# Attention kernel: row sums of weights pass through DRAM with the values, channel means are written to DRAM from their own tile

## The chip, the cores and the metric

The kernel runs on one core of one Trainium2 chip. The metric is the device time of one execution, in microseconds (us). The kernel before takes 2475.26 us, the median of three runs (2474.96 to 2476.18). All data are fp32.

## The reference

Two layers work on `x` of shape 16 x 1024 x 256 (batches, nodes, channels). Layer 0 is a graph layer: x is aggregated over a normalized adjacency, goes through a linear layer, a batch norm, a relu, a second linear layer and a second batch norm, is added to x, and is layer-normed. Layer 1, where the change is made, gates the adjacency by the nodes' channel means, makes queries from it and attends:

```python
fea = jnp.transpose(x, (0, 2, 1))
c_adj = jnp.mean(fea, axis=1)
diff = c_adj[:, None, :] - c_adj[:, :, None]
A = jnp.abs(jnp.abs(jax.nn.sigmoid(diff) - 0.5) - 0.5) * 2.0
A_s = (A + jnp.transpose(A, (0, 2, 1))) * 0.5
Wg = adj[None, :, :] * A_s
g = jnp.einsum('bcn,bnm->bcm', fea, Wg)
g = jax.nn.relu(g * para.reshape(1, C, N))
q = jnp.transpose(g, (0, 2, 1)).reshape(B, N, h, hd).transpose(0, 2, 1, 3)
kv = (x @ kv_w).reshape(B, N, 2, h, hd).transpose(2, 0, 3, 1, 4)
...
attn = jax.nn.softmax(jnp.einsum('bhnd,bhmd->bhnm', q, k) * scale, axis=-1)
out = jnp.einsum('bhnm,bhmd->bhnd', attn, v)
```

The result is added to x and layer-normed again. There are 4 heads of 64 channels.

## The kernel before

Layer 0 ends at about 815 us; the change doesn't touch it. Layer 1 is a software pipeline over 16 batches. A batch has 16 steps, in two halves of 512 queries each, and in each half two pairs of heads. A step makes the scores of 256 keys for one pair and one half (`scores`, L783), their exponentials on ScalarE (`exps`, L795), adds these up for the row sums on VectorE (`sums`, L801 and L804), and multiplies them with the values on TensorE (`attend`, L819).

Work for other batches is put between the steps. `put(b, t, f, ...)` sets a piece of work down for eighth t of batch b. The loop at L1161 takes two eighths at a time, which I call a block: first all pieces of both eighths in the order that `arrange` gives them, then four steps. Four blocks make a batch. In the block of eighths 0 and 1 of batch b lie the first gates, the keys and part of the values of batch b+1 (`gate`, `keys`, `values`) and the row sums of the second half of batch b-1; in that of 4 and 5 the row sums of the first half of batch b; in that of 6 and 7 the means and `crow` of batch b+2. Each engine runs its own instructions strictly in this order; every data transfer of this part is issued by SyncE in this order too, and a transfer that waits holds up those behind it.

Two paths matter here.

*Row sums.* When a half is through, its values (channels x queries, not yet divided) have gone to `o_dram` (L835). `dens` (L840) adds up the partial row sums over the partitions with a matmul against ones (L846), which leaves each head's sums 32 times over in a quarter of the partitions, and ScalarE copies them to DT (L848). `recips` turns them round with four TensorE transposes (L857), and VectorE writes the reciprocals to RD (L859). `fetch_o` (L872) reads the values from DRAM in such an order that VectorE's transpose of 32 x 32 blocks (L890) completes the turn to queries x channels; `finish_a` then multiplies with RD (L894), adds x (L899) and takes the moments of the layer norm, and `finish_b` applies it and writes the output. In most halves `finish_a` comes a block or more after its fetch. In the second half of batch 14 and the first of batch 15 it comes in the same block, the first of them after the third step. The second half of batch 15 (`by_pe`) doesn't pass through DRAM: TensorE transposes it.

*Channel means.* `means` (L674) scales the sums over channels in `css`, a tile of 128 x 8, one node for each number. The gates need them as one row of 1024, the same on all partitions. For the first batch TensorE makes it by transposes (L688). For the others `crow` transposes `css` on TensorE (L692), ScalarE copies the 8 x 128 result into a corner of the tile `crow` (L694), SyncE writes it to `c_dram` (L695), and reads that back to all partitions (L696). The first to read the tile is `wg_a` on ScalarE (L706), at the start of the next block. For batch 1 all this is part of the opening, where TensorE has no other work ahead.

PSUM has four buffers under the tag "t", taken in turn by keys, values, graph products, `pd`, `pr`, `pc` and the two accumulators of `attend`.

Of the kernel before, what the change touches and what calls it, by code (L numbers as in the profile page):

```python
# [22 lines left out]
def gnn_norm_attention_kernel(  # L23
# [57 lines left out]
    Q = 32  # L81
    NQ = P // Q
    y_blk = [yT_all[b].rearrange("i (d e) (q n) -> q e (i d) n", e=Q, q=NQ) for b in range(B)]
    o_dram = {(b, h): dram.tile([NT // NH, C, P], F32, name=f"o{b}_{h}") for b in range(B) for h in range(NH)}
    x1_dram = {
        (b, j): dram.tile([CT, 2 * P, P], F32, name=f"x1_{b}_{j}") for b in range(2, B) for j in range(NT // 2)
    }
# [479 lines left out]
    def fast():  # L567
      with ExitStack() as fx:
# [110 lines left out]
        def crow(b):  # L679


            crows[b] = crp.tile([P, N], F32, tag="crow", name=f"crow_{b}")
            if b == 0:
                for h in range(NH):
                    p = ps_t.tile([P, FB], F32, tag="t", name="pc")
                    for k in range(FB // P):
                        j = h * (FB // P) + k
                        nc.tensor.transpose(p[:, ts(k, P)], css[b][:, j : j + 1].to_broadcast([P, P]), ident)  # L688
                    nc.scalar.copy(crows[b][:, ts(h, FB)], p)
                return  # L690
            p = ps_t.tile([P, FB], F32, tag="t", name="pc")
            nc.tensor.transpose(p[:NT, :P], css[b], ident)  # L692
            t = crows[b][:NT, :P]
            nc.scalar.copy(t, p[:NT, :P])  # L694
            nc.sync.dma_start(c_dram[b], t)  # L695
            nc.sync.dma_start(crows[b], c_dram[b].rearrange("j p -> (j p)").partition_broadcast(P))  # L696


# [112 lines left out]
        def attend(g):  # L811
            b, hf, pair, cp = step(g)
            if cp == 0:
                O[b, hf, pair] = [ps_t.tile([P, FB], F32, tag="t", name=f"o{g}_{r}") for r in range(2)]
            for a in range(2):
                cb = 2 * cp + a
                for r in range(2):
                    for h in range(2):
                        nc.tensor.matmul(  # L819
                            O[b, hf, pair][r][h * HD : (h + 1) * HD, :],  # L820
                            vs[b][r * HD : (r + 1) * HD, cb, pair * P + h * HD : pair * P + (h + 1) * HD],
                            E[g, a][r * HD : (r + 1) * HD, h, :],
                            start=(cb == 0),
                            stop=(cb == NT - 1),
                        )
                E.pop((g, a))
            if cp == NT // 2 - 1:
                t = otp.tile([P, FB], F32, tag=f"ot{pair}", bufs=1, name=f"ot{g}")
                o = O.pop((b, hf, pair))
                nc.scalar.copy(t, o[0])  # L830
                nc.vector.tensor_add(t, o[1], t)  # L831
                if by_pe(b, hf):
                    OT[b, hf, pair] = t
                else:
                    nc.sync.dma_start(  # L835
                        o_dram[b, hf][:, ts(pair, P), :].rearrange("i p n -> p i n"),
                        t.rearrange("p (i n) -> p i n", n=P),
                    )

        def dens(b, hf):  # L840
            p = ps_t.tile([P, FB], F32, tag="t", name="pd")
            for pair in range(NP):
                acc = ACC.pop((b, hf, pair))
                for h in range(2):
                    k = 32 * (2 * pair + h)
                    nc.tensor.matmul(p[k : k + 32, :], ones32, acc[:, h, :], start=True, stop=True)  # L846
            DT[b, hf] = otp.tile([P, FB], F32, tag="dt", bufs=1, name=f"dt{b}_{hf}")
            nc.scalar.copy(DT[b, hf], p)  # L848


        R = {}
# [19 lines left out]

        def fetch_o(b, j):  # L872
            hf, k = divmod(2 * j, KB)
            t = OB[b, j] = otp.tile([P, 2, C], F32, tag="ob", bufs=2, name=f"ob{b}_{j}")
            blk = o_dram[b, hf].rearrange("i (d e) (q n) -> q e (i d) n", e=Q, q=NQ)
            for q in range(NQ):
                nc.sync.dma_start(
                    t[q * Q : (q + 1) * Q].rearrange("p a (d n) -> p (a d) n", n=Q),
                    blk[q][:, ts(k // 2, 2 * C // Q), :],
                )  # L880

        def finish_a(b, j):
            hf, k = divmod(2 * j, KB)
            pool_r = (rp, "r") if b < B - 1 else (x1p, "x1")
            r = pool_r[0].tile([P, 2, C], F32, tag=pool_r[1], name=f"r_{b}_{j}")
            if by_pe(b, hf):
                p = OB.pop((b, j))
            else:
                p = r
                nc.vector.transpose(  # L890
                    r.rearrange("p a c -> p (a c)"), OB.pop((b, j)).rearrange("p a c -> p (a c)")
                )
            rd = RD[:, b * NT + 2 * j : b * NT + 2 * j + 2, :].rearrange("p a h -> p (a h)")
            nc.vector.tensor_mul(  # L894
                r.rearrange("p a (h d) -> p (a h) d", h=HEADS),
                p.rearrange("p a (h d) -> p (a h) d", h=HEADS),
                rd.unsqueeze(2).to_broadcast([P, 2 * HEADS, HD]),
            )
            nc.vector.tensor_add(r, r, x1s.pop((b, j)))  # L899
            mv, rs = ln_stats(sm, r, f"z{b}_{j}")  # L900
            nm = sm.tile([P, 2], F32, tag="nm", name=f"nm_{b}_{j}")
            for a in range(2):
                nc.gpsimd.tensor_scalar(
                    nm[:, a : a + 1], mv[:, a, 0:1], rs[:, a : a + 1], -1.0, op0=OP.mult, op1=OP.mult
                )
            R[b, j] = (r, rs, nm)
# [49 lines left out]
        for b in range(B):  # L956

            for hf in range(NH):
                t = (hf + 1) * (NC // NH)
                put(b, t, dens, b, hf)  # L960
                put(b, t, recips, b, hf)
                for k in range(KB // 2):
                    j = hf * (KB // 2) + k

                    if b * NH + hf < B * NH - 3:
                        t_f, t_a, t_b = (t + 1, t + 2 + k, t + 6 + k) if hf == 0 else (t + 1, t + 4 + k, t + 6 + k)
                    elif not by_pe(b, hf):

                        t_f, t_a, t_b = t, t + 2 * k, t + 2 + 2 * k if b < B - 1 else (t + 2, NC + 1)[k]
                    else:  # L970
                        t_f, t_a, t_b = t, t + 1 + k, t + 2 + k
                    put(b, t_f, back if by_pe(b, hf) else fetch_o, b, j)
                    if t_a == t:
                        between[(b * NC + t) * 2 + NK // 2] = [(finish_a, (b, j))]
                    else:
                        put(b, t_a, finish_a, b, j)
                    put(b, t_b, finish_b, b, j)
# [58 lines left out]
        def arrange(pieces):  # L1036
            first = []
            gates = [fa for fa in pieces if fa[0] is gate]
            many = [fa for fa in pieces if fa[0] in long]
            first += [fa for fa in pieces if fa[0] is bn2_q]  # L1040
            alone = [fa for fa in pieces if fa[0] in (dens, back, recips, crow)]
            few = [fa for fa in pieces if fa not in first + gates + many + alone]
            few.sort(key=lambda fa: rank.get(fa[0], len(rank)))
            few_pe = [fa for fa in few if is_short(fa)]
            order = spread(many, few_pe) if len(many) < len(few_pe) else spread(few_pe, many)
            if few_pe and many and order[0][0] in long:
                order.remove(few_pe[0])
                order.insert(0, few_pe[0])

            for fa in few:  # L1050
                if not is_short(fa):
                    at_ = 0
                    for k, o in enumerate(order):
                        if o[0] in rank and rank[o[0]] <= rank.get(fa[0], len(rank)):
                            at_ = k + 1
                    order.insert(at_, fa)
            if any(fa[0] is graph for fa in many):
                order = gates + order
            else:
                order = spread(order, gates)  # L1060


            for fs, k in (((dens, back), 1), ((recips,), 2)):
                k = ([n for n, fa in enumerate(order) if fa[0] in long] + [len(order)] * 3)[k]
                order[k:k] = [fa for fa in alone if fa[0] in fs]
            return first + order + [fa for fa in alone if fa[0] is crow]


# [278 lines left out]
```

## Time and profile before

| | |
|---|---|
| time, median of 3 | 2475.26 us |
| span of the profiled execution | 2473.1 us |
| PE busy | 98% |
| DVE, ACT, POOL busy | 73%, 44%, 31% |
| DMA moved | 288.66 MB |
| transposes of row sums, L857 | 128, mean 274 ns |
| reciprocals from PSUM, L859 | 32, mean 242 ns; 15.8 us of waiting for `pr` |
| transposes of means, L692 | 15, mean 272 ns |
| fetches of values, L877 | 248 of 64 KB, 2.4 us to landing |
| `crow` broadcast, L696 | 15 of 512 KB, 3.7 us to landing |

PE is TensorE, PEld its weight loads, DVE VectorE, ACT ScalarE, POOL GpSimd, SPq the queue from which SyncE issues transfers. In the timeline, a line has the start of an instruction (or of a run of like ones), its time, engine, line of the kernel, operation, what it writes and reads, and in brackets how long the engine was idle before it and for whom. Names there are of tiles: `pr` is the transposed row sums, `pc` the transposed means, `pk`, `pv` and `pg` are keys, values and graph products, `s` scores, `e` exponentials, `o` attended values, `ob` the values as fetched, `st_d` a small DRAM tensor in which layer 0's last constants `s` and `t` are written at L600 to be fetched in another layout at L602.

### The profile page before, as it was taken

The page shows a single profiled execution, that of the slowest core. Times are in us where ns is not written, and L with a number is a line of the kernel's source. Part 1 is how long each engine was busy: PE and PEld are TensorE (multiplying, and loading weights), DVE is VectorE, ACT ScalarE, POOL GpSimd, SP SyncE. Part 2 cuts the span into 40 slices and gives each one's busy share as a digit, 9 for nine tenths or more (in the row PEclk, how much of TensorE's full clock was granted, in tenths as well). Part 3 has the DMA queues.
Part 4 walks back from the last instruction along what each step waited for, and adds up shares of the span by engine and source line. Part 5 has one row for each costly group of instructions (what it writes and reads, how often), then busy time and mean ns, then how long its engine had stood idle before and what let it go on. Part 6 is the DMA issues. An engine that isn't in the chain of part 4 may idle for free. (4 is left out here: it accounts for less than half of the span.)

```text
span 2473.1 us, 33867 instructions
## 1 busy us (share of the span) xinstructions
PE 2425.5 (98%) x12341; PEld 1021.1 (41%) x12341; DVE 1806.3 (73%) x2552; ACT 1095.1 (44%) x1549; POOL 767.2 (31%) x826
## 2 busy tenths in 40 slices
PE   8999999999999899999999999999999999999997
PEld 4444444444444443443434434344343443443432
DVE  5545545555776777888888878888888888888677
ACT  2000000002544455564655656656566465564645
POOL 2222232321656421313223133232332323414012
PEclk9999999999999899999999999999999999999999
DMA  4122222212677444544544535445354454544211
GB/s 136 68 85 102 78 86 92 102 68 85 226 266 260 125 120 90 129 128 104 141 111 108 144 87 145 116 115 147 76 147 108 118 145 92 135 114 113 65 40 53
DMA packets 563118, 288.66 MB, mean 117 GB/s; under 512 B 390664, under 2 KB 535680, under 8 KB 555776
## 3 DMA queue, kind: packets, MB, share of 16 engines
q1 hardware_dynamic: 562944, 286.43, 42.1%
q8 instruction: 99, 1.62, 0.3%
q14 instruction: 75, 0.61, 0.1%
HBM read 192.43 MB, written 93.91 MB: 116 GB/s over the span
## 5 line engine op out<-in xcount | busy, mean ns | idle before, releaser
L795 ACT ACTIVATE e<-s 128x1024 f32<-128x1024 f32 x512 | 496.1, 1020 | 338.0 <-PE s L783 286.3
L804 DVE TENSOR_TENSOR acc<-acc,e 128x1024 f32<-128x1024 f32 x384 | 517.1, 1347 | 116.6 <-ACT e L795 88.5
L783 PE MATMUL s<-qT,kT 64*64 64x512 f32 x4096 | 492.0, 595 | 3.5 <-ACT e L795 1.5
L819 PE MATMUL o<-e,v 64*64 64x512 f32 x4096 | 485.4, 589 | 0.0
L757 PE MATMUL pg<-wg,x 128*128 128x512 f32 x960 | 428.9, 597 | 0.0
L610 POOL TENSOR_TENSOR yt<-yt,stq 128x512 f32<-128x512 f32 x120 | 181.1, 1510 | 397.9 <-DMA yt<-yT 353.7
L819 PEld LDWEIGHTS o<-e,v 64*64 64x64 f32 x4096 | 156.6, 133 | 282.8 <-issue 274.3
L757 PEld LDWEIGHTS pg<-wg,x 128*128 128x128 f32 x960 | 177.7, 190 | 231.3 <-issue 229.1
L783 PEld LDWEIGHTS s<-qT,kT 64*64 64x64 f32 x4096 | 147.7, 133 | 296.2 <-issue 261.9
L103 ACT COPY u<-pa 128x512 f32<-128x512 f32 x15 | 8.8, 585 | 475.3 <-PE pa L308 475.3
L66 POOL TENSOR_SCALAR rs_z<-mv_z 128x2 f32<-128x2 f32 x64 | 18.3, 286 | 479.2 <-DVE mv_z L559 410.4
L716 DVE SCALAR_TENSOR_TENSOR wg<-wg,adj 128x1024 f32<-128x1024 f32 x128 | 163.5, 1308 | 3.0 <-DMA adj<-in_adj_dram 0.2
L308 PE MATMUL pa<-AhT,x 128*128 128x512 f32 x360 | 161.8, 592 | 0.0
L642 ACT ACTIVATE x<-x,nm_a,rs_a 128x256 f32<-128x256 f32 x128 | 75.8, 594 | 165.8 <-POOL nm_a L632 165.3
L831 DVE TENSOR_TENSOR ot<-o,ot 128x512 f32<-128x512 f32 x64 | 44.3, 692 | 139.2 <-ACT ot L830 139.2
L66 POOL TENSOR_SCALAR rs_a<-mv_a 128x2 f32<-128x2 f32 x64 | 39.4, 616 | 265.3 <-DVE mv_a L559 244.2
L732 PE MATMUL pk<-x1T,kvw 128*128 128x512 f32 x256 | 120.4, 605 | 0.0
L743 PE MATMUL pv<-kvw,x1T 128*128 128x256 f32 x512 | 118.4, 385 | 0.0
L339 PE MATMUL ph<-agg,SW 128*128 128x512 f32 x240 | 112.8, 592 | 0.0
L743 PEld LDWEIGHTS pv<-kvw,x1T 128*128 128x128 f32 x512 | 97.0, 192 | 31.6 <-issue 16.2
L308 PE MATMUL pa<-T,sx 128*128 128x512 f32 x240 | 107.9, 592 | 0.0
L308 PEld LDWEIGHTS pa<-AhT,x 128*128 128x128 f32 x360 | 68.5, 190 | 86.0 <-issue 86.0
(192 smaller groups left out, 3157.4 us busy)
## 6 DMA issues: line engine op xcount, KB each, us to landing
adj<-in_adj_dram SPq DMA_DIRECT2D x128, 512.0 KB, 4.7
h<-hT SPq DMA_DIRECT2D x28, 1024.0 KB, 4.4
hL<-h SPq DMA_DIRECT2D x28, 1024.0 KB, 9.7
x<-in_x_dram SPq DMA_DIRECT2D x16, 1024.0 KB, 7.2
yT<-y SPq DMA_DIRECT2D x64, 256.0 KB, 2.6
out_dram<-r SPq DMA_DIRECT2D x64, 256.0 KB, 2.3
xr<-in_x_dram SPq DMA_DIRECT2D x62, 256.0 KB, 3.5
o<-ot SPq DMA_DIRECT2D x62, 256.0 KB, 2.3
```

The source lines that it names most:

```text
L308: nc.tensor.matmul(p, xs[n][:, k, :], bs[n][:, k, :], start=(k == 0), stop=(k == KN - 1))
L339: nc.tensor.matmul(p, ws[n][:, ts(f, P)], bs[n], start=True, stop=True)
L610: nc.gpsimd.tensor_tensor(y, y, sc, op)
L642: nc.scalar.activation(r, r, AF.Identity, bias=nm[:, a : a + 1], scale=rs[:, a : a + 1], accum_out=css[b][:, i : i + 1])
L716: nc.vector.scalar_tensor_tensor(t, t, 1.0, adjs[b * NT + i], op0=OP.add, op1=OP.mult)
L732: nc.tensor.matmul(p, kvw[:, k, ts(c, P)], x1Ts[b][:, k, ts(h, FB)], start=(k == 0), stop=(k == CT - 1))
L743: nc.tensor.matmul(p[:, ts(a, C)], x1Ts[b][:, k, ts(j + a, P)], kvw[:, k, C:], start=(k == 0), stop=(k == CT - 1),)
L757: nc.tensor.matmul(pg[b], x1s[b, k // 2][:, k % 2, ts(c, P)], wgs[b, k][:, ts(h, FB)], start=(k == 0), stop=(k == NT - 1))
L783: nc.tensor.matmul(t[r * HD : (r + 1) * HD, h, :], kTs[b, pair][h * HD : (h + 1) * HD, ts(2 * cb + r, HD)], qTs[b, pair, hf][h * HD : (h + ...
L795: nc.scalar.activation(E[g, a], S.pop((g, a)), AF.Exp)
L804: nc.vector.tensor_add(ACC[b, hf, pair], ACC[b, hf, pair], E[g, a])
L819: nc.tensor.matmul(O[b, hf, pair][r][h * HD : (h + 1) * HD, :], vs[b][r * HD : (r + 1) * HD, cb, pair * P + h * HD : pair * P + (h + 1) * HD],
```

## The change

It takes transposes off TensorE. The row sums of a half are written below its values: `o_dram` gets 32 more rows (8 for each head, so that the 32 x 32 blocks come out whole), `dens` writes them there from DT with four transfers of 8 partitions, `fetch_o` and the VectorE transpose of `finish_a` carry 288 columns where they carried 256, and `finish_a` takes the reciprocals from the transposed tile, 8 for each of its pieces. `recips` stays for the last half alone. `arrange` puts `dens` ahead of those `fetch_o` that stand in the same block. The means go to `c_dram` straight from `css`, number by number, without the transpose and the copy.

```diff
-    o_dram = {(b, h): dram.tile([NT // NH, C, P], F32, name=f"o{b}_{h}") for b in range(B) for h in range(NH)}
+    DR = 8
+    CD = C + HEADS * DR
+    o_dram = {(b, h): dram.tile([NT // NH, CD, P], F32, name=f"o{b}_{h}") for b in range(B) for h in range(NH)}
...
-            p = ps_t.tile([P, FB], F32, tag="t", name="pc")
-            nc.tensor.transpose(p[:NT, :P], css[b], ident)
-            t = crows[b][:NT, :P]
-            nc.scalar.copy(t, p[:NT, :P])
-            nc.sync.dma_start(c_dram[b], t)
+            with nc.allow_non_contiguous_dma(reason="a thousand numbers"):
+                nc.sync.dma_start(c_dram[b].rearrange("j p -> p j"), css[b])
             nc.sync.dma_start(crows[b], c_dram[b].rearrange("j p -> (j p)").partition_broadcast(P))
...
+        def put_o(b, hf, rows_, t):
+            nc.sync.dma_start(
+                o_dram[b, hf][:, rows_, :].rearrange("i p n -> p i n"), t.rearrange("p (i n) -> p i n", n=P)
+            )
...
             nc.scalar.copy(DT[b, hf], p)
+            if not by_pe(b, hf):
+                for k in range(HEADS):
+                    put_o(b, hf, slice(C + k * DR, C + (k + 1) * DR), DT[b, hf][32 * k : 32 * k + DR, :])
...
-            t = OB[b, j] = otp.tile([P, 2, C], F32, tag="ob", bufs=2, name=f"ob{b}_{j}")
+            t = OB[b, j] = otp.tile([P, 2, CD], F32, tag="ob", bufs=2, name=f"ob{b}_{j}")
...
-                    blk[q][:, ts(k // 2, 2 * C // Q), :],
+                    blk[q][:, ts(k // 2, 2 * CD // Q), :],
...
-            pool_r = (rp, "r") if b < B - 1 else (x1p, "x1")
-            r = pool_r[0].tile([P, 2, C], F32, tag=pool_r[1], name=f"r_{b}_{j}")
+            pool_r = (rp, "r") if b < B - 1 or not by_pe(b, hf) else (x1p, "x1")
+            rd = RD[:, b * NT + 2 * j : b * NT + 2 * j + 2, :]
             if by_pe(b, hf):
+                r = pool_r[0].tile([P, 2, C], F32, tag=pool_r[1], name=f"r_{b}_{j}")
                 p = OB.pop((b, j))
             else:
-                p = r
+                t = pool_r[0].tile([P, 2, CD], F32, tag=pool_r[1], name=f"r_{b}_{j}")
                 nc.vector.transpose(
-                    r.rearrange("p a c -> p (a c)"), OB.pop((b, j)).rearrange("p a c -> p (a c)")
+                    t.rearrange("p a c -> p (a c)"), OB.pop((b, j)).rearrange("p a c -> p (a c)")
                 )
+                nc.vector.reciprocal(rd, t[:, :, C:].rearrange("p a (h r) -> p a h r", r=DR)[:, :, :, 0])
+                p = r = t[:, :, :C]
...
-                put(b, t, recips, b, hf)
+                if by_pe(b, hf):
+                    put(b, t, recips, b, hf)
...
+            if any(fa[0] is dens for fa in alone):
+                k = [fa[0] for fa in order].index(dens)
+                late = [fa for fa in order[:k] if fa[0] is fetch_o]
+                order = [fa for fa in order[:k] if fa not in late] + [order[k]] + late + order[k + 1 :]
```

More of the change, by code (lines that the diff above doesn't have):

```diff
@@ L834, in attend @@
                 else:
[L835 to L838, printed above, removed]
+                    put_o(b, hf, slice(pair * P, (pair + 1) * P), t)
+        def put_o(b, hf, rows_, t):
+            nc.sync.dma_start(
+                o_dram[b, hf][:, rows_, :].rearrange("i p n -> p i n"), t.rearrange("p (i n) -> p i n", n=P)
+            )
         def dens(b, hf):
@@ L883, in finish_a @@
             hf, k = divmod(2 * j, KB)
-            pool_r = (rp, "r") if b < B - 1 else (x1p, "x1")
-            r = pool_r[0].tile([P, 2, C], F32, tag=pool_r[1], name=f"r_{b}_{j}")
+            pool_r = (rp, "r") if b < B - 1 or not by_pe(b, hf) else (x1p, "x1")
+            rd = RD[:, b * NT + 2 * j : b * NT + 2 * j + 2, :]
             if by_pe(b, hf):
+                r = pool_r[0].tile([P, 2, C], F32, tag=pool_r[1], name=f"r_{b}_{j}")
                 p = OB.pop((b, j))
             else:
-                p = r
+                t = pool_r[0].tile([P, 2, CD], F32, tag=pool_r[1], name=f"r_{b}_{j}")
                 nc.vector.transpose(
-                    r.rearrange("p a c -> p (a c)"), OB.pop((b, j)).rearrange("p a c -> p (a c)")
+                    t.rearrange("p a c -> p (a c)"), OB.pop((b, j)).rearrange("p a c -> p (a c)")
                 )
-            rd = RD[:, b * NT + 2 * j : b * NT + 2 * j + 2, :].rearrange("p a h -> p (a h)")
+                nc.vector.reciprocal(rd, t[:, :, C:].rearrange("p a (h r) -> p a h r", r=DR)[:, :, :, 0])
+                p = r = t[:, :, :C]
             nc.vector.tensor_mul(
-                r.rearrange("p a (h d) -> p (a h) d", h=HEADS),
-                p.rearrange("p a (h d) -> p (a h) d", h=HEADS),
-                rd.unsqueeze(2).to_broadcast([P, 2 * HEADS, HD]),
+                r.rearrange("p a (h d) -> p a h d", h=HEADS),
+                p.rearrange("p a (h d) -> p a h d", h=HEADS),
+                rd.unsqueeze(3).to_broadcast([P, 2, HEADS, HD]),
             )
```

## The prediction

> **What bounds the kernel now.** I read the busy shares first, then the tensor engine's timeline around the two kinds of transposes that go, then the waits. The page opens with
>
> ```profile
> PE 2425.5 (98%) x12341; PEld 1021.1 (41%) x12341; DVE 1806.3 (73%) x2552; ACT 1095.1 (44%) x1549; POOL 767.2 (31%) x826
> ```
>
> and a query by stretches gives, for one whole batch of the attention part,
>
> ```profile
> 1053.44:1154.84 101.40, 101.27 (x653) 40.99 (x650) 83.96 (x113) 59.07 (x82) 31.21 (x40) 1.00 0.48 120
> ```
>
> (columns: stretch, its length, then PE, PEld, DVE, ACT, POOL busy, clock, DMA share, GB/s). PE is busy 101.27 of 101.40 us at full clock, so an instruction less on PE shortens the batch unless another engine becomes late. The chain of waits holds one step, an ACT one, and tells nothing here.
>
> The timeline of PE prices the two removals. Beside the recips (L857), and around the crow transpose (L692), with the same place in the last batch, where there is no crow:
>
> ```profile
> 979.46 1.98 PE L732 MATMUL pk<-x1T,kvw 128*128 128x512 f32 x4
> 981.28 0.60 PE L857 MATMUL pr<-ident,dt 128*128 128x128 f32 x4
> 981.71 3.60 PE L732 MATMUL pk<-x1T,kvw 128*128 128x512 f32 x8
> ...
> 1053.44 10.57 PE L757 MATMUL pg<-wg,x 128*128 128x512 f32 x24
> 1063.85 0.27 PE L692 MATMUL pc<-ident,cs 128*8 128x128 f32 x1
> 1064.05 1.95 PE L783 MATMUL s<-qT,kT 64*64 64x512 f32 x16
> ...
> 2371.59 10.57 PE L757 MATMUL pg<-wg,x 128*128 128x512 f32 x24
> 2382.09 1.95 PE L783 MATMUL s<-qT,kT 64*64 64x512 f32 x16
> ```
>
> The reader is to read starts, not durations: the ends overlap.
>
> What the change adds is a write of 1024 single numbers to DRAM, and what waits behind it. The SyncE queue now, beside ACT, which reads crow first at 1078.53:
>
> ```profile
> 1067.33 0.33 SPq L695 DMA_DIRECT2D crow_d<-crow  x1
> 1069.16 0.34 SPq L696 DMA_DIRECT2D crow<-crow_d  x1
> ...
> 1078.53 2.19 ACT L706 ACTIVATE wg<-crow,hcs 128x1024 f32<-128x1024 f32 x2
> 1080.62 0.57 ACT L735 COPY kT<-pk 128x512 f32<-128x512 f32 x1
> 1081.09 0.59 ACT L848 COPY dt<-pd 128x512 f32<-128x512 f32 x1
> 1082.88 0.58 ACT L735 COPY kT<-pk 128x512 f32<-128x512 f32 x1 [1.20 <-PE pk L732]
> ...
> 1088.47 0.58 ACT L750 COPY v<-pv 128x512 f32<-128x512 f32 x1 [0.93 <-PE pv L743]
> ```
>
> The only writes of single numbers in the kernel, 256 each, are those of s2 and t2, with the fetch that waits for both:
>
> ```profile
> 813.77 0.37 SPq L600 DMA_DIRECT2D st_d<-s  x1
> 814.23 0.42 SPq L600 DMA_DIRECT2D st_d<-t  x1
> 822.57 0.86 SPq L602 DMA_DIRECT2D stq<-st_d  x2
> ```
>
> [...] st_d<-s, 1 KB, takes 8.1 us to land, while 4 KB of crow_d in rows of 512 B let its reader start 1.83 us after. [...] here fetch_o starts 2.3 us after the put of ot (2397.43 to 2399.75). [...]
>
> **The change part by part.**
>
> *Recips off PE.* Of 32 groups of four transposes 31 go (the last half keeps its own). Matmuls there run at (985.15-981.71)/8 = 0.43 us each, so the four from 979.46 end their turn at 981.18, and the next starts at 981.71: a group costs 0.53. Beside graph matmuls it is the same (929.79 to 931.19 for two of 0.43 and a group). 29 groups lie in full blocks: 29 x 0.53 = 15.4 us off.
>
> *The two late groups* (the second half of batch 14, the first of batch 15): PE there waits for dt as well, 2396.99 to 2398.34 and 2428.35 to 2430.14, 1.35 + 1.79 = 3.1 us. Most returns: fetch_o must now wait for four puts of dt. dt is there at 2397.7; four issues at 0.45 and 2.3 to land put the fetch at 2401.8 instead of 2399.75, the first block lands 4.4 later at 2406.2, and finish_a, which DVE takes up at 2406.46 now, would have been taken up at 2405.1. DVE is then full until the end (the sum of exps runs to 2457.6 and PE waits 0.66 us for it). Ends 0 and 3.1; I take 0.5.
>
> *crow's transpose off PE.* With it 1053.44 to 1064.05 is 10.61; without it 10.50. 14 x 0.11 = 1.5 us. ACT's copy (254 ns x15) goes too, in idle time: ACT waited 107.3 us in all for it, but its next work, the exps, needs the scores that come after it on PE.
>
> *The write of single numbers.* Call W the time from its issue to the issue of the broadcast. st_d<-s needs 8.1; st_d<-t, issued with it in flight, 8.3 until the waiting fetch starts. A second 256 numbers in flight did not make the second slower, so I take the cost as a latency that many numbers share: W = 8.3. Ends: 1.8 (as now) and, if it grows with the numbers in flight, 0.8 + (8.3-0.8) x 1024/512 = 15.8.
> Deadline: the broadcast takes 3.7 to land, so for 1078.53 it must be issued at 1074.8, 7.5 after 1067.33. DVE reaches the transpose that frees the queue some 0.5 later (two finish_a), and the block is 0.1 shorter: 6.9. Beyond it ACT waits, with the copies of kT, dt and v queued behind, then the exps, which PE's scores need. ACT has 1.20 idle before the second kT and 0.93 before v, of which 0.53 goes as PE comes earlier: 1.6 in all. So a batch pays nothing up to W = 8.5, and each us beyond is paid 14 times. At 8.3 it is hidden by that idle time, barely.
> *At the opening* there is no slack: cs is ready at 872.4, ACT takes crow at 878.55, 4.2 after the broadcast's issue, and works without a gap to the exps at 888.31, which PE waits for. The new crow is there at 872.4 + 8.3 + 4.2 = 884.9: 6.4 us on. PE's own wait for cs (3.04) goes, but only to wait later for those exps.
>
> *DVE.* The transpose has 64 columns more (62 x 64 x 0.97 ns = 3.9 us, slope from 692 at 512 to 1189 at 1024), 62 reciprocals at about 0.17 (the 128x8 hcs takes 172) are 10.5, and 31 x 0.242 = 7.5 go: +6.9 us over 16 batches, and 15.8 us of waits for pr go. It hides: in the batch above DVE is 84 of 101.4.
>
> *DMA.* 124 puts (16 KB each), 18 segments for 16 in fetch_o. Fetches begin about 2 to 4 us later, and x1 puts and yt loads queue behind; finish_a comes a block (25 us) after its fetch, except in the late halves. Nothing.
>
> Sum: -15.4 - 1.5 - 0.5 + 6.4 = -11.0: **2464.3 us**.
>
> **The rivals.**
> *Quick write.* The 8 us of st_d are special to that spot; W about 4 costs 2.1 at the opening: 2475.3 - 17.4 + 2.1 = 2460.0. For it: the packets of both writes are through within about 1 us. Against: nothing else was in the way, since the puts of y had landed.
> *Near the edge.* W = 9.3, as 768 more packets may add 1 us: opening 7.4, batches 14 x 0.8 = 11.2: 2476.5, no change. DVE showing its 6.9 us would land near it too (2471).
> *A new wait in each batch.* W = 10 gives 8.1 + 21: 2487. If W grows with the numbers, 15.8: opening 13.9, batches 14 x 7.3 = 102: 2574, clearly slower. For it: 8 us for 1 KB is long[...]. Against: the second write's 8.3.
>
> **How the numbers follow.** Hidden write 0.42 (2464), quick write 0.18 (2460), edge 0.10 (2476), W of 9.6 to 11 0.14 (2481 to 2502), scaled 0.16 (2574). Faster 0.42 + 0.18 = 0.60, same 0.10, slower 0.30. The range 2457 to 2503 leaves out the scaled case and little else.
>
> **What would show it.** A batch of about 101.4 - 2 x 0.53 - 0.11 = 100.2 us if the write is hidden. crow<-crow_d issued about 8.3 after crow_d<-cs. The first wg of a batch waiting for crow by under 1.5 us, at the opening by some 6. No pr but in the last half, DVE no longer waiting at L859. Wrong if ACT's wait for crow is over 2 us in each batch, or if DVE's waits for ob grow.

## The result, and the profile after

The changed kernel takes 2498.77 us (median of four runs, 2497.23 to 2501.28), the one before 2475.72 beside it (2474.96 to 2476.21): ratio 1.0094, 95% interval 1.0077 to 1.0112. It is slower by 23 us; forecast was 11 us faster. The profiled span is 2495.6 us, before it was 2473.1. The page now opens with

```profile
PE 2416.2 (97%) x12202; PEld 1006.4 (40%) x12202; DVE 1811.0 (73%) x2583; ACT 1089.0 (44%) x1534; POOL 771.2 (31%) x826
```

PE lost 139 instructions and 9.3 us of busy time, as a change that takes work off PE should. But what is left of the span when busy time is taken off went from 2473.1 - 2425.5 = 47.6 to 2495.6 - 2416.2 = 79.4 us. The work went, and 32 us of waiting came. The same stretch of a batch as before, from the start of the graph products of one block to that of the next batch (columns: stretch, length, then PE, PEld, DVE, ACT and POOL busy, clock, DMA share, GB/s):

```profile
1063.77:1166.93 103.16, 100.54 (x644) 40.01 (x640) 84.82 (x116) 58.63 (x81) 30.64 (x40) 1.00 0.50 121
```

PE has 100.54 us to do, 0.73 less than before, and the batch is 103.16 long, 1.76 longer. Who waits, by the table of waits (in all, times, longest):

```profile
ACT wg L707 <- DMA crow<-crow_d: 63.8, 15, 13.8
...
PE s L784 <- ACT e L796: 22.9, 17, 2.3
PE pv L744 <- ACT kT L736: 9.5, 1, 9.5
...
PE pk L733 <- ACT kT L736: 6.0, 8, 1.3
```

In each of the 15 batches that write `css` number by number, ScalarE stands at the first `wg` until the broadcast has landed: 13.77 us at the opening and 50.0 in the 14 others, 3.57 each. The three PE lines are where TensorE waits in turn; 3.0 us of the first of them stand at the end of the kernel, as they do in e5 and e6 below without the slow write. How it gets there is seen in one batch of the timeline (SyncE's queue, ScalarE and PE, by time):

```profile
1078.21 0.49 SPq L696 DMA_DIRECT2D crow_d<-cs  x1
1089.09 0.34 SPq L697 DMA_DIRECT2D crow<-crow_d  x1
...
1090.08 1.06 PE L849 MATMUL pd<-acc,ones 128*32 128x512 f32 x8
1091.07 3.70 PE L733 MATMUL pk<-x1T,kvw 128*128 128x512 f32 x8
...
1093.38 2.19 ACT L707 ACTIVATE wg<-crow,hcs 128x1024 f32<-128x1024 f32 x2 [4.53 <-DMA crow<-crow_d]
1095.48 0.56 ACT L736 COPY kT<-pk 128x512 f32<-128x512 f32 x1
...
1096.10 1.98 PE L733 MATMUL pk<-x1T,kvw 128*128 128x512 f32 x4 [1.32 <-ACT kT L736]
...
1104.69 2.00 PE L784 MATMUL s<-qT,kT 64*64 64x512 f32 x16 [1.29 <-ACT e L796]
```

The write of the means is issued at 1078.21 and the broadcast that waits for it at 1089.09: W, the prediction's name for this time, is 10.88 us here. ScalarE takes up `wg` 4.29 later, and the copy of `kT` queued behind it ends too late for the next `pk`, which has no PSUM buffer: 1.32 us of PE. The rest comes back at the scores, 1.29. No `pr` stands behind `pd` any more, so that part of the change did what it was for.

At the opening PE has nothing else to do, and nearly the whole wait arrives:

```profile
873.76 0.38 SPq L696 DMA_DIRECT2D crow_d<-cs  x1
884.10 0.33 SPq L697 DMA_DIRECT2D crow<-crow_d  x1
...
888.59 1.15 ACT L707 ACTIVATE wg<-crow,hcs 128x1024 f32<-128x1024 f32 x1 [13.77 <-DMA crow<-crow_d]
...
890.26 3.78 PE L744 MATMUL pv<-kvw,x1T 128*128 128x256 f32 x8 [9.47 <-ACT kT L736]
```

The first `wg` is 10.04 later than before (878.55). Of this, 1.35 was there already in the work ahead of the opening (its last group of transposes starts at 870.23 against 868.88). That start differs between the traces of this case, from 868.33 to 870.35, whether the kernel has the change or not. The opening itself lost 8.7. The waiting broadcast also holds up what SyncE issues after it: four fetches of `yt` go out at 884.51, where the kernel before has them at 874.78.

### The profile page after: what moved, and what is told of

It is laid out like the page before. It is cut to its first block, busy times and chain, and to the rows that moved or that the text cites. A ratio compares the mean times of both kernels' runs of the same rounds, so it can differ in the third digit from the quotient of the medians.

```text
span 2495.6 us, 33800 instructions
## 1 busy us (share of the span) xinstructions
PE 2416.2 (97%) x12202; PEld 1006.4 (40%) x12202; DVE 1811.0 (73%) x2583; ACT 1089.0 (44%) x1534; POOL 771.2 (31%) x826
## 5 line engine op out<-in xcount | busy, mean ns | idle before, releaser
L805 DVE TENSOR_TENSOR acc<-acc,e 128x1024 f32<-128x1024 f32 x384 | 508.6, 1324 | 119.4 <-ACT e L796 93.2
L614 POOL TENSOR_TENSOR yt<-yt,stq 128x512 f32<-128x512 f32 x120 | 174.4, 1454 | 455.2 <-DMA yt<-yT 395.0
L707 ACT ACTIVATE wg<-crow,hcs 128x1024 f32<-128x1024 f32 x80 | 89.1, 1153 | 63.8 <-DMA crow<-crow_d 63.8
```

Source lines behind the costliest of these rows:

```text
L614: nc.gpsimd.tensor_tensor(y, y, sc, op)
L707: nc.scalar.activation(t, crows[b], AF.Tanh, bias=hcs[b][:, i : i + 1], scale=-0.5)
L805: nc.vector.tensor_add(ACC[b, hf, pair], ACC[b, hf, pair], E[g, a])
```

## Experiments

My theory after the result: the rows through DRAM gain what was forecast, and all the loss is the write of 1024 single numbers. Its rival: the rows cost something too (four more transfers for each half, fetches that start later), and the two share the loss. In the text a kernel goes by the start of its label, e1 to e10. The unmodified kernel took 2476.41 to 2477.02 us beside these runs (medians).

**The two parts alone.** In the first, `crow` is as before and the rows go through DRAM; in the second, the reverse.

```diff
 e1_rows_only (from the changed kernel)
-            with nc.allow_non_contiguous_dma(reason="a thousand numbers"):
-                nc.sync.dma_start(c_dram[b].rearrange("j p -> p j"), css[b])
+            p = ps_t.tile([P, FB], F32, tag="t", name="pc")
+            nc.tensor.transpose(p[:NT, :P], css[b], ident)
+            t = crows[b][:NT, :P]
+            nc.scalar.copy(t, p[:NT, :P])
+            nc.sync.dma_start(c_dram[b], t)
 e2_means_only (from the kernel before): the reverse of these lines
```

> Row sums through DRAM as in the changed kernel, channel means transposed on TensorE as before. Theory 1 (the loss is all in the write of single numbers and what waits for crow; the row-sum part does what was forecast): 15.4 us for 29 groups and about 1 for the two late ones off 2475.7, so 2459 to 2461. Theory 2 (the fetches behind the puts of dt, the longer VectorE work and the queue behind them are what costs; the wait for crow only shows where the delay ends): 2485 or more.

> The kernel before with only the means written number by number. Theory 1: 8 to 9 us at the opening, a wait for crow of some 3 us in each batch of which about 2 are absorbed by ScalarE's idle time there, less 1.5 for the transposes that go: 2492 to 2505. Theory 2: within 5 us of before, 2470 to 2480.

Rows only: 2462.42 us, ratio 0.9947 (0.9929 to 0.9964), 14.0 faster and an us above what I expected. Means only: 2524.8, ratio 1.0203 (1.0184 to 1.0223), 48.4 slower, 20 beyond the range that I expected. So the rows only gain and the rival falls. The two don't add up, though: 48.4 - 14.0 = 34.4, and together they cost 23. The waits of the second kernel say why:

```profile
ACT wg L703 <- DMA crow<-crow_d: 57.2, 15, 14.4
...
PE pr L854 <- ACT dt L845: 30.6, 16, 4.1
```

With the recips still on PE, `pr` needs `dt`, and ScalarE's copy of `dt` is queued behind the `wg` that waits for crow. PE stands there 30.6 us. Taking the recips off PE removes that meeting point, so the first part of the change shelters the second.

**The same write, earlier.** The means are ready some time before `crow` is reached in SyncE's queue: eight fetches of x1 lie between. Here the write is issued as soon as `css` is scaled, in `means`, for all batches but the first; only the broadcast stays in `crow`.

```diff
 in means:
             nc.vector.tensor_scalar_mul(hcs[b], css[b], 0.5)
+            if b > 0:
+                with nc.allow_non_contiguous_dma(reason="a thousand numbers"):
+                    nc.sync.dma_start(c_dram[b].rearrange("j p -> p j"), css[b])
 in crow:
-            with nc.allow_non_contiguous_dma(reason="a thousand numbers"):
-                nc.sync.dma_start(c_dram[b].rearrange("j p -> p j"), css[b])
```

> The changed kernel with the same write of single numbers issued some 7 us sooner, right after the means, ahead of the fetches of x1 in SyncE's queue; the broadcast stays where it is. Theory 1: the write is through when SyncE comes to the broadcast, crow lands in time in every batch but at the opening, where nothing changes: about 30 us off 2498.8, 2466 to 2470. If the slow write holds up the fetches that now follow it in the DMA queues, the gain is smaller, and the transposes of x1 on VectorE show a wait for them. Theory 2: no change, 2495 to 2502.

It takes 2473.49 us, ratio 0.9988 (0.9979 to 0.9997), 25.3 less than the changed kernel, but 3.5 above the range of theory 1. Waits for crow are 17.8 us, of which 13.9 at the opening, where no time lies ahead. The queue shows a price that isn't ScalarE's:

```profile
1067.39 0.36 SPq L684 DMA_DIRECT2D crow_d<-cs  x1
...
1068.48 12.12 SPq L664 DMA_DIRECT2D xb<-x  x8
1080.65 0.49 SPq L698 DMA_DIRECT2D crow<-crow_d  x1
```

The eight fetches issued behind the write occupy SyncE for 12.12 us; in e5 below, with no slow write ahead of them, the eight take 7.53. The longest of the 224 issues of such fetches takes 6.53 us in e3, and 1.86 in the kernel before; the median is 0.49 in both. The write seems to hold up what is queued behind it. The transposes of x1 on VectorE show no wait for these fetches; where the missing 3.5 us may have gone is taken up with e10 below.

**The write measured by itself.** Writes of several forms at the end of the kernel before, one after another, each followed by a fetch of one number that waits for it, in one execution. Rows are 128 of 32 B; the others are single numbers of 4 B, either side by side in DRAM or apart.

```diff
+ one_("r32",   [P, 8],        the tile as it is,               8 columns)
+ one_("n128",  [1, P],        "j p -> p j",                    1 column)
+ one_("n256"), ("n512"), ("n1024"), ("n2048"): the same with 2, 4, 8, 16 columns
+ one_("s64",   [8, P * 16],   every 16th number, "j p -> p j", 8 columns)
+ one_("s512",  [8, P * 128],  every 128th number,              8 columns)
```

> The kernel before, and at its end, where nothing else moves, a chain of writes to DRAM, each followed by a fetch of one number that waits for it, twice over: 128 rows of 32 B, then 128, 256, 512, 1024 and 2048 single numbers next to each other in DRAM, then 1024 numbers each 64 B and each 512 B from the next. Latency theory (numbers in flight share the wait): 8 to 10 us for all counts. Count theory: doubling from count to count, 1024 at 10, 2048 at 20. Sharing theory (numbers that share a stretch of DRAM wait for one another): the spread writes are through in 2 to 4 us at the same count of 1024. Rows of 32 B: 2 to 4 us if the count of pieces matters[...].

The second round of them, each write with the fetch that waited for it (SyncE's queue; `pd_r` rows, `pd_n` neighbouring numbers, first 128 and then 1024 of them, `pd_s` 1024 numbers 64 B apart):

```profile
2528.16 0.33 SPq L954 DMA_DIRECT2D pd_r<-psrc  x1
2529.56 0.23 SPq L956 DMA_DIRECT2D pt_r<-pd_r  x1
2529.84 0.33 SPq L954 DMA_DIRECT2D pd_n<-psrc  x1
2537.79 0.23 SPq L956 DMA_DIRECT2D pt_n<-pd_n  x1
...
2555.78 0.36 SPq L954 DMA_DIRECT2D pd_n<-psrc  x1
2566.11 0.23 SPq L956 DMA_DIRECT2D pt_n<-pd_n  x1
...
2577.98 0.36 SPq L954 DMA_DIRECT2D pd_s<-psrc  x1
2580.57 0.23 SPq L956 DMA_DIRECT2D pt_s<-pd_s  x1
```

| write, 4-byte numbers | from issue to the waiting fetch, two rounds, us |
|---|---|
| 128 rows of 8 neighbours | 3.0 (of which 1.7 is the issue), 1.40 |
| 128 single, side by side | 7.78, 7.95 |
| 256 | 8.30, 8.50 |
| 512 | 9.71, 8.65 |
| 1024 | 10.40, 10.33 |
| 2048 | 10.96, 11.30 |
| 1024 single, 64 B apart | 2.57, 2.59 |
| 1024 single, 512 B apart | 2.91, 2.50 |

Neither the count nor being single makes the write slow: 1024 single numbers 64 B apart are through in 2.6 us, 128 neighbours need 7.8. Nor is it the sending of the pieces. The next lines cut two writes of the second round into the time in which the numbers are sent and the time left until the waiting fetch, first for the 1024 neighbours, then for the 1024 that lie 64 B apart (columns as above; the last two are DMA share and GB/s):

```profile
2555.78:2557.78 2.00, 0.00 (x0) 0.00 (x0) 0.00 (x0) 0.00 (x0) 0.00 (x0) 0.50 0.30 6
2557.78:2566.11 8.33, 0.00 (x0) 0.00 (x0) 0.00 (x0) 0.00 (x0) 0.00 (x0) 0.50 0.00 0
2577.98:2579.78 1.80, 0.00 (x0) 0.00 (x0) 0.00 (x0) 0.00 (x0) 0.00 (x0) 0.50 0.26 2
2579.78:2580.57 0.79, 0.00 (x0) 0.00 (x0) 0.00 (x0) 0.00 (x0) 0.00 (x0) 0.50 0.00 0
```

In both, all transfer that is recorded lies in the first 2 us. Behind the neighbours another 8.3 us pass, in which nothing is recorded to move, until the fetch that waits for them can be issued; behind the numbers apart it is 0.8. The 256 numbers of layer 0, from which I took W, are here at 8.3 to 8.5, as forecast; at 1024 it is 10.4.

**A write that nobody waits for.** From e1: the quick `crow` of before, and ahead of its write the slow one, to a tensor that nothing reads. If only the wait for the slow write cost time, it would be free.

```diff
+            with nc.allow_non_contiguous_dma(reason="read by nobody"):
+                nc.sync.dma_start(x_dram[b].rearrange("j p -> p j"), css[b])
             nc.sync.dma_start(c_dram[b], t)
```

> e1_rows_only, where crow goes the old way, plus the write of 1024 single numbers to a DRAM tensor that nobody reads, issued just before. Theory 1 (only the wait for the write costs): within 2 us of e1_rows_only, 2461 to 2465. Rival (the slow write holds up whatever comes after it in the DMA queues): the broadcast behind it lands some 6 us later, 2470 or more.

2489.94 us (2486.88 to 2493.67), ratio 1.0057 (1.004 to 1.0073): 27.5 above e1.

```profile
1078.18 0.49 SPq L701 DMA_DIRECT2D xtra_d<-cs  x1
1078.77 0.42 SPq L702 DMA_DIRECT2D crow_d<-crow  x1
1088.37 0.34 SPq L703 DMA_DIRECT2D crow<-crow_d  x1
```

The write of eight rows of 512 B, which let its reader start 1.83 us after in the kernel before, now takes 9.60. So the slow write holds up the quick one behind it, though no instruction waits for its own result.

**The same, spread.** The extra write of e7 with each number 512 B from the next, nothing else.

```diff
-                nc.sync.dma_start(x_dram[b].rearrange("j p -> p j"), css[b])
+                nc.sync.dma_start(
+                    x_dram[b].rearrange("j (p z) -> p j z", z=P)[:, :, 0:1], css[b].unsqueeze(2)
+                )
```

> The kernel that does the rows part alone (2462.4), with the same write of 1024 single numbers that nobody reads ahead of the write of rows, only that each number now goes 512 B from the next in DRAM. If a write of single numbers is slow because neighbours in DRAM wait for one another, this one is over in about 2.6 us and holds up next to nothing: 2461 to 2465, the write of rows reaches its reader within 2 to 4 us, waits for crow under 5 us in all. If it is the count of single numbers that holds up the queue behind them: about 2490, as with the numbers side by side.

2462.46 us (2461.98 to 2462.95), ratio 0.9943 (0.9926 to 0.996), the time of e1 within 0.1.

```profile
1068.81 0.50 SPq L701 DMA_DIRECT2D xtra_d<-cs  x1
1069.40 0.42 SPq L704 DMA_DIRECT2D crow_d<-crow  x1
1071.92 0.34 SPq L705 DMA_DIRECT2D crow<-crow_d  x1
```

The rows behind it reach their reader after 2.52 us, and the waits for crow come to 1.6 us in all. As many numbers and as many bytes, 27 us apart in the whole: it is where they lie.

**The opening alone.** The changed kernel, with `crow` of batch 1 made by TensorE as that of batch 0 is (`if b == 0` becomes `if b <= 1` in `crow`).

> The changed kernel with crow of batch 1 alone made on TensorE like that of batch 0; all later batches as changed. Theory 1: the 8 to 9 us of the opening come back and the waits of the 14 later batches stay: 2488 to 2491. If the opening's loss only moves the later work and is taken up there, no difference from 2498.8.

2483.09 us (2481.4 to 2484.84), ratio 1.0029 (1.0017 to 1.004): 15.7 less than the changed kernel, more than expected. The starts of the first `pd` lie 10.4 us apart in the two profiles (-0.31 to the kernel before, instead of +10.05), but 1.9 of that is the work ahead of the opening, which happened to start early here (868.33). The opening itself is worth 8.5. The other 5.5 us arise in the batches: W averages 9.47 over the 14 of them where it was 9.84, and W and landing together 0.28 less, 14 x 0.28 = 3.9. That W differs so between runs is seen, not explained, and the remaining 1.6 aren't either.

**Early write and opening together.** The edits of e3 and e8 in one kernel.

> The changed kernel with the write of the means issued right after they are made, ahead of the fetches of x1, and the column of batch 1 still made by TensorE. If the slow write is wholly hidden when it has the time of the fetches, what is left of its cost is the opening alone, and taking that away gives 2473.5 - 10.4, about 2463 (2461 to 2465), with waits for crow under 5 us. If fetches that land late cost something of their own (PE waiting for x1T), 2466 to 2472.

2463.21 us (2461.88 to 2464.91), ratio 0.9945 (0.9928 to 0.9961); waits for crow 3.6 us. Against e3 it gains 10.3 in the medians; 8.5 of this is the opening, read from the profiles as for e8 (the 10.4 that went into the expectation was too much). So nearly all of the slow write is hidden when the time of the fetches lies ahead. But e6 below, with the same opening and no slow write, takes 3.0 us less. In the profile of e10, TensorE falls 4.4 us behind e6, all of it in two batches, and in both an `exps` on ScalarE starts late (another 4.69 at 1877.36):

```profile
1172.42 1.94 ACT L797 ACTIVATE e<-s 128x1024 f32<-128x1024 f32 x2 [5.03 <-remote]
```

"remote" is a release for which the profile knows no instruction. Such waits stand in e3 and e10 alone, the two kernels with the early write; e3, too, loses 4.8 us against e5 at the three places where it has them. What ScalarE waits for there isn't known.

**Another way off TensorE.** VectorE's transpose of 32 x 32 blocks (0.21 us at this size, in e5) turns a zeroed 128 x 32 tile with the means in its first 8 columns; four writes of 8 rows of 128 B take them to DRAM. In the second kernel `crow` of batch 1 is made by TensorE as well.

```diff
 e5_block_transpose (from the changed kernel)
-            with nc.allow_non_contiguous_dma(reason="a thousand numbers"):
-                nc.sync.dma_start(c_dram[b].rearrange("j p -> p j"), css[b])
+            cw, ct = CW[:, 0, :], CW[:, 1, :]
+            nc.vector.tensor_copy(cw[:, :NT], css[b])
+            nc.vector.transpose(ct, cw)
+            for q in range(NQ):
+                nc.sync.dma_start(c_dram[b][:, ts(q, Q)], ct[q * Q : q * Q + NT, :])
 e6_block_and_opening: this, and
-            if b == 0:
+            if b <= 1:
```

> The changed kernel with the means turned by VectorE: copied into a 128 x 32 tile that is zero elsewhere, its 32 x 32 blocks transposed, and written to DRAM as rows of 128 B with four transfers, in the place of the write of single numbers. Theory (neighbouring single numbers make the write slow): the broadcast is issued 3 to 4 us after the first write, in time in every batch; 1.5 us less than e1_rows_only for the transposes of means and some 2 more at the opening: 2461 to 2464. [...]

> As e5_block_transpose, and crow of batch 1 made on TensorE like that of batch 0, without DRAM. Theory: the opening has no wait for crow at all and is about 1 us shorter than in the kernel before: 2458 to 2461, the fastest of all. If the opening's cost was not the wait for crow, no difference from e5_block_transpose.

The first takes 2462.07 us, ratio 0.9944 (0.9927 to 0.996), with one wait for crow, 6.2 us at the opening; the second 2460.2 (2459.24 to 2460.53), ratio 0.9934 (0.9917 to 0.995), with none. It is the fastest measured here, ahead of both kernels. Its queue and its page:

```profile
1067.98 1.34 SPq L701 DMA_DIRECT2D crow_d<-CW  x4
1070.26 0.35 SPq L702 DMA_DIRECT2D crow<-crow_d  x1
```

```profile
PE 2411.3 (98%) x12210; PEld 1008.6 (41%) x12210; DVE 1811.3 (74%) x2611; ACT 1091.5 (44%) x1536; POOL 766.0 (31%) x827
```

The broadcast follows the first of the four writes by 2.28 us, and TensorE is 47.3 us short of busy, as in the kernel before. VectorE's two small instructions, 0.16 and 0.21 us in e5, cost nothing that shows.

## Why the prediction was wrong, step by step

**The step that failed: "I take the cost as a latency that many numbers share: W = 8.3."** Measured W is 9.84 on average in the 14 batches (8.19 to 11.15) and 10.34 at the opening. Two writes of 256 weren't evidence for one of 1024: by itself a write of 256 takes 8.3 to 8.5 and one of 1024 10.4, so four times the count adds about 2 us, and the threshold stood at 8.5. Nor is it a latency of many numbers as such: 1024 of them 64 B apart take 2.6. The range of W, 1.8 to 15.8, was honest; the value was set 0.2 below the edge, where an error upwards costs 14 times and one downwards nothing. The result lies where the prediction put W of 9.6 to 11, with a chance of 0.14, and its sign of being wrong came true: ScalarE waits for crow for 3.57 us in a batch, over the 2 named.

**The landing of the broadcast, 3.7**, was the page's median of landings. What was wanted is the time from issue to the start of the waiting `wg`. The only place in the trace before where that could be read, the opening, gave 4.2, and the prediction used it there and not for the batches. Measured, the mean of 14 is 4.44.

Both terms are of one sum. The threshold was W + landing = 8.5 + 3.7 = 12.2; measured is 9.84 + 4.44 = 14.28, so by the prediction's own sum 2.1 us a batch should come through, 14 x 2.1 = 29. Measured: e5 has the same work on TensorE in these batches and no wait for crow in them, and from the first `pd` to the thirtieth the changed kernel falls 27.8 us behind it, 1.99 a batch. ScalarE's wait is 3.57, so 1.6 of it is taken up, where **the idle time of 1.6 on ScalarE** was forecast. That step holds.

**The opening, +6.4**, is 8.7: W 2.0 more and landing 0.3 more. The steps named, down to the exps that PE waits for, are the ones in the trace.

**Recips, "a group costs 0.53".** It is 0.435: in e1 the start of `pd` moves ahead by 0.43 or 0.44 with each half, 12.20 us from the second to the thirtieth (28 groups). The transposes take their 0.43 like other matmuls (981.28 to 981.71 in the lines shown). The other 0.1 belongs to the first matmuls behind `pd`, and stays there with no transposes: in the changed kernel the first matmul behind a `pd` still takes 0.54 until the next one starts (1041.95 to 1042.49), and that one 0.43 (to 1042.92). I had put on the group a cost that its neighbour has. Instead of 15.4 it is 29 x 0.435 = 12.6.

**crow's transpose, 1.5, the late groups, 0.5.** The first is confirmed: in e5, where it is off PE too, alternate halves gain 0.55 and 0.44. The second is within what can be told: e1 gained 14.0 where 12.6 and 0.5 stand.

**DVE, "+6.9, it hides".** DVE is busy 1811.0 for 1806.3, 4.7 more. e1 has that work and only gains. **DMA, "Nothing"** was right of the fetches and puts of the rows (e1). But I looked only at more bytes and issues and not at what the slow write does to transfers behind it. e7 shows that it holds them, 9.60 for 1.83; in the changed kernel the broadcast stands next behind the write and waits for it in any case, and the sum below has no term for what comes later in the queue, so that this error cost the forecast nothing that shows.

With the measured terms the sum nearly closes: 2475.3 - 12.6 - 1.5 - 0.5 + 8.7 + 27.8 = 2497.2; measured 2498.8. The 1.6 left are about what the work ahead of the opening adds in the profiled run (1.35), which isn't in the sum. Of the rivals the nearest was W = 10 with 2487; it lacked the longer landing (14 x 0.7 = 10) and the smaller gain of the recips. The scaled one, 2574, my estimate of a W that grows with the count, falls with the probe: from 256 to 2048 numbers W grows by a third.

**What stays open.** Why neighbours are slow. 1024 numbers 64 B apart are through in 2.6 us, and 128 rows of 32 B that touch in 1.4. Whether neighbours wait because they share a small stretch of DRAM, or because they all lie in one region (128 of them span 512 B, 1024 span 4 KB), the probe doesn't divide; that the 128 rows span 4 KB, too, and take 1.4 us speaks against the region alone. Small pieces by themselves don't make a write slow: four writes in rows of 128 B let their reader start 2.28 us after the first (e6), rows of 32 B take 1.4, and 1024 pieces of 4 B take 2.5 to 2.9 apart and 10.4 side by side. What passes in the 8.3 us in which no transfer is recorded wasn't shown. Not tried: the slow write from another engine's queue, and `crow` itself written with its numbers apart.

## To carry to other kernels

Read the time of a DRAM write from its issue to the issue of the transfer that waits for it, and of the same shape; a write of neighbouring single numbers can take several times as long as rows or as numbers apart (10.4 us against 1.4 and 2.6 here), and it stretches what is queued behind it (9.60 us for 1.83). Where a forecast has a threshold that is paid once per loop, an estimate at its edge is a coin toss, and the likeliest time should be worked out from the middle of the range of the unknown. The gain of removing an instruction is the spacing from its own start to the next one's, not what a stretch loses with it if its neighbours have a start-up of their own (0.435 us here, for 0.53).

## What the runs showed of the hardware

- 1024 numbers of 4 B side by side in DRAM: 10.4 us until a reader could be issued; 64 B apart 2.6; 128 rows of 32 B 1.4. Already 128 side by side take 7.8 (all in e4). The numbers are sent within 2 us side by side and 64 B apart; in the 8.3 us that follow for the neighbours no transfer is recorded.
- A transfer behind such a write waits with it: eight rows of 512 B take 9.6 us in e7 instead of 1.8 in the kernel before, and eight fetches of x1 occupy SyncE for 12.1 in e3 instead of 7.5 in e5. Behind a spread write of as many numbers the eight rows take 2.5 (e9).
- W of the same write ranged from 8.19 to 11.15 within one execution of the changed kernel, and its mean over 14 batches was 9.47 in e8 and 9.84 in the changed kernel.
